# An attention block's opening: x transposed raw, mean and rstd spread by transposes, rstd applied to the first query product

## The chip, the cores and the metric

The kernel runs on one core of a Trainium2 chip. The core has five engines with queues of their own: TensorE (PE; its weight loads are shown apart as PEld), VectorE (DVE), ScalarE (ACT), GpSimd (POOL) and SyncE (SP), which here issues nearly all DMA transfers. Each engine takes its instructions in the order written and waits on semaphores for the others. The metric is the time of one execution on the device in microseconds; runs of the kernel before gave a median of 568.15 us (three runs, 568.02 to 568.37).

## What is computed

Cross attention with a layer norm in front, in float32, for a batch of 8 sequences of 256 rows of width 1024, 32 heads of 32:

```python
mu, var = mean(x), var(x)                       # over the last axis, of 1024
xn = (x - mu) * rsqrt(var + 1e-5) * gamma + beta
Q = split_heads(xn @ Wq.T)                      # 32 heads of 32
K = V = split_heads(ctx)                        # the memory is used for both
probs = softmax(where(mask, Q @ K.T / sqrt(32), -inf))
out = x + merge_heads(probs @ V) @ Wout.T
```

## The kernel before

All shapes are cut into tiles of 128 partitions. A sequence `b` of 256 rows is two halves `s`; the width of 1024 is eight chunks `c` of 128; the query has eight tiles `o` of 128 columns, each holding four heads. The unit of work is `n = 8 * b + o`, 64 in all: a query tile, its scores (four heads, one PSUM bank each, tag `sc`, four banks in all), a softmax, the values, and the output projection of the sequence before. The whole order is written by hand: each engine's queue holds its instructions in the order in which the Python code emits them.

The norm: `ln_stats` (line 217) takes two `bn_stats` of 512 columns and a `bn_aggr` on VectorE, adds epsilon, and raises to the power -0.5 on GpSimd (line 235). `ln_norm` (line 242) subtracts the mean and multiplies by rstd on the rows. PE then transposes the rows (x is the stationary operand, the identity or a diagonal matrix the moving one), since the query product contracts over the width. Gamma and beta differ by column of x, so after the transpose they are one number per partition. The query tile carries one more column (S, the 257th) that holds what beta gives; it serves as the bias of the queries of the later sequences, for which gamma and the scale are folded into `wq` (`fold`, line 364).

The opening, which the change touches, is sequence 0 and stands after line 876:

- 32 dummy transposes of the identity into a spare bank (line 119), before any data are there.
- Loads on SP's queue: rows of half 0 in two pieces, rows of half 1, `wq` tile 0, the keys, the mask, rows of sequence 1, further `wq` tiles; gamma and beta are loaded from ScalarE's queue (line 193).
- Half 0: statistics (line 227); the mean is subtracted by VectorE from the first 512 columns (line 882) and by GpSimd from the rest (line 885); rstd stands in a diagonal matrix (line 884), and the transposes of line 273 are products with that matrix, which apply rstd. `copy_x0` (lines 280 and 282) evacuates them with gamma and beta. `first_q(0)` (line 290) makes the first query tile's half, copied with the scale by line 294.
- Half 1: statistics, `ln_norm` on VectorE (line 253), plain transposes (line 271), the same evacuation, `first_q(1)`.
- The scores of half 0 (line 486), then two chunks of query tile 1 (`make_q`, line 345), then the scores of half 1, then the other chunks of tile 1 and tile 2. VectorE takes maxima with the mask (line 524), ScalarE exponentials (line 528), GpSimd the normalization (line 543). VectorE also takes the statistics of sequence 1 between the two halves' maxima.

Of the kernel before, what the change touches and what calls it, by code (L numbers as in the profile page):

```python
# [46 lines left out]
F32 = mybir.dt.float32  # L47
# [4 lines left out]
P = 128  # L52
# [7 lines left out]
def xattn_kernel(  # L60
# [54 lines left out]


    busy = ps_s.tile([P, P], F32, tag="sc", name="busy")
    for _ in range(32):
        nc.tensor.transpose(busy, ident, ident)


    xs, ks, vs, rs = {}, {}, {}, {}
# [68 lines left out]

    nc.scalar.activation(gs[:, :NS], mhalf, AF.Exp)
    nc.scalar.dma_start(gb, gamma_beta)
    load_x(0, 0, 0)
    load_x(0, 0, 1)
    load_x(0, 1)
    load_wq(0)
    load_k(0)
    load_mask(0)
    load_x(1, 0)  # L200
    load_wq(1)
    load_x(1, 1)
    for o in range(2, 5):
        load_wq(o)
# [12 lines left out]
    def ln_stats(b, s, parts=range(3), later=None):  # L217


        if s == 0 and 0 in parts:  # L220
            mvs[b] = sm.tile([P, NS, 2], F32, tag="mv", name=f"mv_{b}", bufs=2)
            rstds[b] = sm.tile([P, NS], F32, tag="rstd", name=f"rstd_{b}", bufs=2)
        if 0 in parts:
            sts[b, s] = sm.tile([P, 2, 6], F32, tag="st", name=f"st_{b}_{s}", bufs=2)
        for h in range(2):
            if h in parts:
                nc.vector.bn_stats(sts[b, s][:, h, :], xs[b][:, s, ts(h, 512)])
        if 2 not in parts:
            return
        nc.vector.bn_aggr(mvs[b][:, s, :], sts[b, s].rearrange("p h k -> p (h k)"))  # L230
        ve = sm.tile([P, 1], F32, tag="ve", name=f"ve_{b}_{s}", bufs=2)
        nc.vector.tensor_scalar(ve, mvs[b][:, s, 1:2], LN_EPS, None, ALU.add)

        def pow_():
            nc.gpsimd.tensor_tensor(rstds[b][:, s : s + 1], ve, mhalf[:, :1], ALU.pow)

        if later is None:
            pow_()
        else:
            later.append(pow_)  # L240
# [14 lines left out]
            ALU.subtract, ALU.mult,  # L255
        )

    xnT0 = lnp.tile([P, NC, S + 1], F32, tag="xnT", name="xnT_0")
    xnTs[0] = lambda c: xnT0[:, c, :]
    px0 = {}  # L260

    def transpose_x0(s, diag=None):

        pool, tag, k = (ps_v, "pv", NC // 2) if diag is None else (ps_s, "sc", 2)
        for g in range(NC // k):
            pt = pool.tile([P, k, P], F32, tag=tag, name=f"px0_{s}_{g}")
            for i in range(k):
                px0[s, k * g + i] = pt[:, i, :]
                chunk = xs[0][:, s, ts(k * g + i, P)]
                if diag is None:  # L270
                    nc.tensor.transpose(pt[:, i, :], chunk, ident)
                else:
                    nc.tensor.matmul(pt[:, i, :], chunk, diag, start=True, stop=True)  # L273

    def copy_x0(s, c, engine):

        to, pt = xnT0[:, c, ts(s, P)], px0[s, c]
        g, b = gam[:, c : c + 1], bet[:, c : c + 1]
        if engine is nc.scalar:
            nc.scalar.activation(to, pt, AF.Identity, bias=b, scale=g)  # L280
        else:
            nc.vector.tensor_scalar(to, pt, g, b, ALU.mult, ALU.add)

    def first_q(s, chunks=range(NC)):

        if s == 0:
            pqs[0] = ps_q.tile([P, 512], F32, tag="pq", name="pq_0")
        cols = ds(0, P) if s == 0 else ds(P, P + 1)
        for c in chunks:
            nc.tensor.matmul(  # L290
                pqs[0][:, cols], wq[:, 0, c, :], xnT0[:, c, cols],
                start=(c == chunks[0]), stop=(c == chunks[-1]),
            )
        nc.scalar.activation(qa[:, 0, cols], pqs[0][:, cols], AF.Copy, scale=NEG_SCALE)

    xes, px1 = {}, {}

# [51 lines left out]
    def copy_q(n):  # L349
        b, o = divmod(n, NQ)  # L350
        if b == 0:
            nc.scalar.activation(qa[:, o], pqs.pop(n), AF.Copy, scale=NEG_SCALE)
        elif b == 1:
            nc.scalar.activation(
                qa[:, o, :S], pqs.pop(n), AF.Identity, bias=qa[:, o, S : S + 1],
            )
        else:
            nc.scalar.activation(
                qa[:, o, :S].rearrange("p (s a k) -> p a s k", s=NS, a=NA),
                pqs.pop(n).rearrange("p (a s k) -> p a s k", s=NS, a=NA),  # L360
                AF.Identity, bias=qa[:, o, S : S + 1],
            )
# [113 lines left out]
        nc.vector.tensor_scalar(mbs[b], mks.pop(b), 1.0, -MASKED, ALU.subtract, ALU.mult)  # L476

    def scores(n, part=range(NS)):
        if 0 in part:
            scs[n] = [  # L480
                ps_s.tile([P, NS, T], F32, tag="sc", name=f"sc_{n}_{j}") for j in range(NH)
            ]
        for s in part:
            for j in range(NH):
                r = slice(j * HD, (j + 1) * HD)
                nc.tensor.matmul(  # L486
                    scs[n][j][:, s, :], qa[r, n % NQ, ts(s, P)], ks[n - n % 2][r, n % 2, :],
                    start=True, stop=True,
                )
# [10 lines left out]
    def softmax_parts(n, copies=(), ahead=(), between=(), hooks={}, fill=()):  # L500
# [14 lines left out]
        es, mns, dens = {}, {}, {}  # L515

        def exps(j, part=range(NS)):
            if 0 in part:
                es[j] = ep.tile([P, NS, T], F32, tag="e", name=f"e_{n}_{j}")
                mns[j] = sm.tile([P, NS], F32, tag="mn", name=f"mn_{n}_{j}")  # L520
                dens[j] = sm.tile([P, NS], F32, tag="den", name=f"den_{n}_{j}")
# [34 lines left out]

        if n == 0:
            for j in range(NH - 1):
                exps(j, (0,))
            yield  # L560
            exps(NH - 1, (0,))
            fill_in()
            yield
            for j in range(NH):
                exps(j, (1,))
            normalize(0)
            fill_in()
        else:
# [307 lines left out]
                    rings[slot].append(partial(load_ring, name, half))  # L876


    ln_stats(0, 0)
    x0 = xs[0][:, 0, :]  # L880
    mean = mvs[0][:, 0, 0:1]
    nc.vector.tensor_scalar(x0[:, :512], x0[:, :512], mean, None, ALU.subtract)
    diag = ring[:, 0, 1, :]
    nc.vector.tensor_scalar(diag, ident, rstds[0][:, 0:1], None, ALU.mult)
    nc.gpsimd.tensor_scalar(x0[:, 512:], x0[:, 512:], mean, 1.0, ALU.subtract, ALU.mult)  # L885
    ln_stats(0, 1)
    transpose_x0(0, diag)
    early, late = (0, 1, 2, 3, 6, 7), (4, 5)
    for c in early + late:
        copy_x0(0, c, nc.vector if c > 5 else nc.scalar)  # L890
    nc.gpsimd.tensor_copy(xnT0[:, :, S], bet)
    ln_norm(0, 1, nc.vector)
    first_q(0, early + late)
    mask_bias(0)
    transpose_x0(1)
    scores(0, (0,))
    for c in range(NC):
        copy_x0(1, c, nc.scalar if c < NC // 2 else nc.vector)
    first = softmax_parts(0, (partial(copy_q, 1), partial(copy_q, 2)), (), (), {}, [
        partial(ln_stats, 1, 0), partial(ln_stats, 1, 1),  # L900
        partial(ln_norm, 1, 0, nc.vector),
    ])
    next(first)
    first_q(1)
    make_q(1, second=True, chunks=range(2))
    next(first)
    scores(0, (1,))
    make_q(1, second=True, chunks=range(2, NC))
    make_q(2)
    for _ in first:  # L910
        pass
    ln_norm(1, 1, nc.vector)
    nc.gpsimd.tensor_scalar(gs, gam, NEG_SCALE, 1.0, ALU.mult, ALU.mult)
    for o in range(2):
        fold(o)

# [246 lines left out]
```

## Time and profile before

| | |
|---|---|
| median of three runs | 568.15 us (568.02 to 568.37) |
| span of the profiled execution | 566.0 us |
| TensorE busy | 561.4 us |
| VectorE, ScalarE, GpSimd busy | 467.6, 423.4, 394.3 us |
| DMA moved | 119.02 MB, mean 210 GB/s |

The span runs from the first to the last instruction; a run's time also has what lies around it. A row of the profile gives the engine, the line of the kernel, the operation, the tile written and the tile read, shapes, the number of instructions, then busy time and mean duration; after a bar stands the idle time of the engine before it and what ended it. Instructions of an engine overlap, so that a duration is not the distance to the next one. A float32 product is two records on PE, a transpose one.

### The profile page before, as it was taken

The page shows a single profiled execution, that of the slowest core. Times are in us where ns is not written, and L with a number is a line of the kernel's source. Part 1 is how long each engine was busy: PE and PEld are TensorE (multiplying, and loading weights), DVE is VectorE, ACT ScalarE, POOL GpSimd, SP SyncE. Part 2 cuts the span into 40 slices and gives each one's busy share as a digit, 9 for nine tenths or more (in the row PEclk, how much of TensorE's full clock was granted, in tenths as well). Part 3 has the DMA queues.
Part 4 walks back from the last instruction along what each step waited for, and adds up shares of the span by engine and source line. Part 5 has one row for each costly group of instructions (what it writes and reads, how often), then busy time and mean ns, then how long its engine had stood idle before and what let it go on. Part 6 is the DMA issues. An engine that isn't in the chain of part 4 may idle for free.

```text
span 566.0 us, 20200 instructions
## 1 busy us (share of the span) xinstructions
PE 561.4 (99%) x7266; PEld 393.7 (70%) x7266; DVE 467.6 (83%) x1716; ACT 423.4 (75%) x1464; POOL 394.3 (70%) x636
## 2 busy tenths in 40 slices
PE   8999999999999999999999999999999999999997
PEld 8788886767766767667766776667766767755454
DVE  5889889999988988878898888988888777879923
ACT  4699999997778866786777876778776776769820
POOL 2788887899777656857568665777648657448780
PEclk9999999999999999999999999999999999999999
DMA  8966667856697777966778767796658864536751
GB/s 310 397 181 199 185 198 228 281 162 179 212 301 232 223 202 235 263 195 191 233 216 239 215 176 221 230 273 193 176 140 269 255 191 128 146 110 180 218 156 74
DMA packets 47219, 119.02 MB, mean 210 GB/s; under 512 B 8976, under 2 KB 9744, under 8 KB 47120
## 3 DMA queue, kind: packets, MB, share of 16 engines
q1 hardware_dynamic: 46976, 117.74, 69.5%
q8 instruction: 57, 0.93, 0.8%
q14 instruction: 42, 0.34, 0.2%
q10 hardware_dynamic: 144, 0.01, 0.0%
HBM read 66.33 MB, written 11.53 MB: 138 GB/s over the span
## 4 chain that ended last, share of the span: by engine, by line
PE 97%; DMA 1%; DVE 0%; POOL 0%; ACT 0%; issue 0%; SPq 0%; POOLq 0%
PE po_S L720 21%; PE pq_A L447 19%; PE pv L636 12%; PE sc L486 12%; PE po_A L720 11%; PE pq L345 9%; PE pq_S L447 8%; PE po_end L787 3%; PE po_last L787 1%; DMA x<-in_x_dram 1%; PE po_end_s L787 0%; POOL x L885 0%; PE pq L290 0%; PE px L307 0%; ACT e L528 0%; PE px L273 0%
## 5 line engine op out<-in xcount | busy, mean ns | idle before, releaser
L543 POOL TENSOR_SCALAR e<-e,rden 128x256 f32<-128x256 f32 x466 | 215.4, 479 | 125.5 <-DVE rden L535 123.0
L528 ACT ACTIVATE e<-e,mn 128x256 f32<-128x256 f32 x512 | 254.0, 502 | 46.1 <-DVE mn L524 44.9
L549 DVE STREAM_TRANSPOSE pT<-e 128x512 f32<-128x512 f32 x256 | 178.9, 703 | 35.6 <-POOL e L543 27.5
L524 DVE CUSTOM_DVE_ANT_0 e<-sc,mb 128x256 f32<-128x256 f32 x512 | 185.3, 415 | 25.4 <-PE sc L486 25.1
L555 ACT COPY pc<-pT 128x512 f32<-128x512 f32 x128 | 79.0, 617 | 55.7 <-DVE pT L549 35.6
L528 ACT ACTIVATION_READ_ACCUMULATOR e<-e,mn 128x1 f32 x512 | 98.4, 192 | 0.0
L486 PEld LDWEIGHTS sc<-k,qa 32*128 32x128 f32 x1024 | 46.1, 184 | 42.2 <-issue 21.6
L720 PE MATMUL po_S<-wo,at 128*128 128x512 f32 x152 | 74.3, 606 | 0.0
L636 PE MATMUL pv<-pT,v 64*32 64x128 f32 x4096 | 74.1, 274 | 0.0
L486 PE MATMUL sc<-k,qa 32*128 32x256 f32 x1024 | 73.6, 401 | 0.1
L636 PEld LDWEIGHTS pv<-pT,v 64*32 64x32 f32 x4096 | 57.0, 105 | 22.5 <-issue 11.8
L720 PE MATMUL po_A<-wo,at 128*128 128x512 f32 x128 | 59.4, 605 | 0.0
L345 PE MATMUL pq<-xnT,wq 128*128 128x256 f32 (+1 forms) x240 | 55.0, 384 | 0.0
L447 PEld LDWEIGHTS pq_A<-xnT,wq 128*128 128x128 f32 x416 | 48.5, 192 | 6.2 <-issue 4.8
L345 PEld LDWEIGHTS pq<-xnT,wq 128*128 128x128 f32 x240 | 44.6, 190 | 8.2 <-issue 1.5
L720 PE MATMUL po_S<-wo,s 128*128 128x512 f32 x104 | 50.1, 606 | 0.0
L447 PE MATMUL pq_A<-xnT,wq 128*128 128x128 f32 x416 | 48.5, 275 | 0.0
L535 DVE RECIPROCAL rden<-den 128x2 f32<-128x2 f32 x256 | 38.2, 150 | 7.3 <-ACT e L528 6.2
L524 DVE DVE_READ_ACCUMULATOR2_ANT mn<- 128x1 f32 x512 | 42.4, 83 | 0.0
L720 PEld LDWEIGHTS po_A<-wo,at 128*128 128x128 f32 x128 | 22.9, 189 | 25.6 <-issue 24.5
L720 PEld LDWEIGHTS po_S<-wo,at 128*128 128x128 f32 x152 | 25.5, 190 | 19.5 <-issue 19.5
L753 POOL TENSOR_TENSOR r<-r,p 128x512 f32<-128x512 f32 x24 | 30.6, 1277 | 4.8 <-ACT e L528 3.0
(102 smaller groups left out, 666.1 us busy)
## 6 DMA issues: line engine op xcount, KB each, us to landing
v<-in_kv_dram SPq DMA_DIRECT2D x32, 512.0 KB, 4.2
pT<-pT SPq DMA_DIRECT2D x128, 128.0 KB, 2.9
pT<-pc SPq DMA_DIRECT2D x128, 128.0 KB, 4.0
ring<-kept_T SPq DMA_DIRECT2D x20, 512.0 KB, 5.3
k<-in_kv_dram SPq DMA_DIRECT2D x32, 256.0 KB, 4.1
x<-in_x_dram SPq DMA_DIRECT2D x15, 512.0 KB, 5.6
r<-in_x_dram SPq DMA_DIRECT2D x28, 256.0 KB, 4.5
out_dram<-r SPq DMA_DIRECT2D x28, 256.0 KB, 3.2
```

Source lines behind the costliest of these rows:

```text
L345: nc.tensor.matmul(pqs[n], wq[:, o, c, :], xnTs[b](c), start=(c == 0), stop=(c == NC - 1),)
L447: nc.tensor.matmul(pqs[b][:, o, :], w[:, c], x_[:, c], start=begins and o + c == 0, stop=c == NK - 1, skip_group_check=True,)
L486: nc.tensor.matmul(scs[n][j][:, s, :], qa[r, n % NQ, ts(s, P)], ks[n - n % 2][r, n % 2, :], start=True, stop=True,)
L524: nc.vector.tensor_tensor_reduce(out=e[:, s, :], in0=pss[j][:, s, :], in1=mbs[n // NQ], scale=1.0, scalar=NO_SCORE, op0=ALU.add, op1=ALU.m ...
L528: nc.scalar.activation(e[:, s, :], e[:, s, :], AF.Exp, bias=mn[:, s : s + 1], scale=-1.0, accum_out=den[:, s : s + 1],)
L535: nc.vector.reciprocal(rden, dens[j])
L543: engine.tensor_scalar(es[j][:, s, :], es[j][:, s, :], rden[:, s : s + 1], 1.0, ALU.mult, ALU.mult,)
L549: nc.vector.transpose(pT[:, :, :, j, :, :].rearrange("p a i s k -> p (a i) s k"), es[j].rearrange("p s (b t) -> p b s t", t=K),)
L555: nc.scalar.copy(pc[:, :, ts(j, 2)], pT[:, 1, :, ts(j, 2)])
L636: nc.tensor.matmul(pvs[n][r][j * HD : (j + 1) * HD], vs[n - n % 2][ts(r, 2 * K), i, ds(n % 2 * P + j * HD, HD)], pT[ts(r, 2 * K), :, i, j, ...
L720: nc.tensor.matmul(po, operand(b, name)[:, c], wo[:, which, c], start=begins and c == 0, stop=c == NK - 1, skip_group_check=not begins,)
L753: nc.gpsimd.tensor_tensor(r, r, p1s[b], ALU.add)
```

## The change

The opening of sequence 0 is written anew:

- The half s=1 is loaded, normalized and used first, then s=0. The second `wq` tile is loaded ahead of the rows of sequence 1.
- Of the 32 dummy transposes 6 stay at the start; 10 more stand in groups of 2, 2, 3 and 3 between the real ones.
- The rows are transposed as they land, without mean or rstd. A column of 128 means (or rstds), read with its one column repeated 128 times, is transposed as well (`spread`): each partition then holds the row of all means. ScalarE copies it out of PSUM (`keep_mean`, `keep_rstd`) into a buffer that is free until later (`sums_x`).
- VectorE subtracts the means while it takes the transposed rows out of PSUM, 512 columns at a time (`centre_x0`). Gamma with the negative scale is multiplied in place, 16 chunks of 128x128, twelve by ScalarE and four by VectorE (`gamma_x0`). This is `xcT0`.
- The first query product (`first_q`) reads `xcT0`, so rstd is still missing; `take_q` multiplies the product by the row of rstds on VectorE and adds the bias on ScalarE. For the other query tiles `scale_x0` makes `xnT0` from `xcT0` times rstd, three quarters of it on GpSimd and one on VectorE.
- `copy_q` of sequence 0 becomes two ScalarE instructions: the bias column, and the queries with that bias. The scale factor `gs` is computed at the start instead of ahead of the folds.

The diff, cut to its core:

```diff
-    for _ in range(32):
-        nc.tensor.transpose(busy, ident, ident)
+    def keep_busy(times):
+        for _ in range(times):
+            nc.tensor.transpose(busy, ident, ident)
+    keep_busy(6)
...
-    load_x(0, 0, 0)
-    load_x(0, 0, 1)
-    load_x(0, 1)
+    load_x(0, 1, 0)
+    load_x(0, 1, 1)
+    load_x(0, 0)
     load_wq(0)
     load_k(0)
     load_mask(0)
+    load_wq(1)
     load_x(1, 0)
-    load_wq(1)
     load_x(1, 1)
...
+    rows = sums_x.rearrange("p i c a k -> p (i c a k)")
+    rows0, means0 = rows[:, :S], rows[:, ds(S, S)]
+    def transpose_x0(s, g):
+        px0[s, g] = ps_v.tile([P, NC // 2, P], F32, tag="pv", name=f"px0_{s}_{g}")
+        for i in range(NC // 2):
+            chunk = xs[0][:, s, ts(NC // 2 * g + i, P)]
+            nc.tensor.transpose(px0[s, g][:, i, :], chunk, ident)
+    def spread(s, what):
+        if what == 0:
+            stat0[s] = ps_o.tile([P, 2, P], F32, tag="po", name=f"stat0_{s}")
+        one = mvs[0][:, s, 0:1] if what == 0 else rstds[0][:, s : s + 1]
+        nc.tensor.transpose(stat0[s][:, what, :], one.to_broadcast([P, P]), ident)
+    def keep_mean(s):
+        nc.scalar.copy(means0[:, ts(s, P)], stat0[s][:, 0, :])
+    def centre_x0(s, g):
+        nc.vector.tensor_tensor(
+            xcT0[:, ts(g, NC // 2), ts(s, P)], px0[s, g],
+            means0[:, ts(s, P)].unsqueeze(1).to_broadcast([P, NC // 2, P]), ALU.subtract,
+        )
+    def gamma_x0(s, c, engine):
+        it, g = xcT0[:, c, ts(s, P)], gs[:, c : c + 1]
         if engine is nc.scalar:
+            nc.scalar.activation(it, it, AF.Copy, scale=g)
         else:
+            nc.vector.tensor_scalar(it, it, g, None, ALU.mult)
+    def keep_rstd(s):
+        nc.scalar.copy(rows0[:, ts(s, P)], stat0[s][:, 1, :])
+    def scale_x0(s, g, engine):
+        engine.tensor_tensor(
+            xnT0[:, ts(g, NC // 2), ts(s, P)], xcT0[:, ts(g, NC // 2), ts(s, P)],
+            rows0[:, ts(s, P)].unsqueeze(1).to_broadcast([P, NC // 2, P]), ALU.mult,
+        )
+    QUERY_0 = (0, 1, 2, 3, 4, 6, 5, 7)
...
+    def take_q(o, bank, cols):
+        to = qa[:, o, cols]
+        nc.vector.tensor_tensor(to, bank[:, cols], rows0[:, cols], ALU.mult)
+        nc.scalar.activation(to, to, AF.Identity, bias=qa[:, o, S : S + 1])
...
-            nc.scalar.activation(qa[:, o], pqs.pop(n), AF.Copy, scale=NEG_SCALE)
+            bank = pqs.pop(n)
+            take_bias(o, bank)
+            nc.scalar.activation(
+                qa[:, o, :S], bank[:, :S], AF.Identity, bias=qa[:, o, S : S + 1],
+            )
...
+    def gammas(s):
+        for c in QUERY_0:
+            gamma_x0(s, c, nc.vector if s == 0 and c in (2, 4, 6, 7) else nc.scalar)
+    nc.gpsimd.tensor_scalar(gs, gam, NEG_SCALE, 1.0, ALU.mult, ALU.mult)
+    for to in (xcT0, xnT0):
+        nc.gpsimd.tensor_scalar(to[:, :, S], bet, NEG_SCALE, 1.0, ALU.mult, ALU.mult)
+    ln_stats(0, 1)
+    transpose_x0(1, 0)
+    keep_busy(2)
+    transpose_x0(1, 1)
+    keep_busy(2)
+    spread(1, 0)
+    keep_busy(3)
+    spread(1, 1)
+    keep_busy(3)
+    keep_mean(1)
+    keep_rstd(1)
+    centre_x0(1, 0)
+    centre_x0(1, 1)
+    gammas(1)
+    scale_x0(1, 0, nc.gpsimd)
     ln_stats(0, 0)
+    scale_x0(1, 1, nc.gpsimd)
+    transpose_x0(0, 0)
+    transpose_x0(0, 1)
+    first_q(1, QUERY_0[:5])
+    spread(0, 0)
+    first_q(1, QUERY_0[5:])
+    spread(0, 1)
+    keep_mean(0)
+    centre_x0(0, 0)
+    centre_x0(0, 1)
+    take_bias(0, pqs[0])
+    gammas(0)
+    keep_rstd(0)
+    take_q(0, pqs[0], slice(P, S))
+    scale_x0(0, 0, nc.vector)
+    scale_x0(0, 1, nc.gpsimd)
     mask_bias(0)
+    first_q(0)
+    scores(0, (1,))
+    take_q(0, pqs[0], slice(0, P))
...
-    first_q(1)
     make_q(1, second=True, chunks=range(2))
     next(first)
-    scores(0, (1,))
+    scores(0, (0,))
     make_q(1, second=True, chunks=range(2, NC))
     make_q(2)
```

64 lines of the change are left out of this document (16 added, 48 removed).

## The prediction

> **What bounds the kernel now.** I read the page first, then busy time by stretches, then the chain of waits in order of time. The page says that TensorE (PE) works nearly all of the span and that the chain that ends last is PE too.
>
> ```profile
> span 566.0 us, 20200 instructions
> PE 561.4 (99%) x7266; PEld 393.7 (70%) x7266; DVE 467.6 (83%) x1716; ACT 423.4 (75%) x1464; POOL 394.3 (70%) x636
> PE 97%; DMA 1%; DVE 0%; POOL 0%; ACT 0%; issue 0%; SPq 0%; POOLq 0%
> ```
>
> By stretches (columns: stretch, its length, busy us and records of PE, weight loads, VectorE, ScalarE, GpSimd, then granted clock, DMA share, GB/s):
>
> ```profile
> 0.00:20.00 20.00, 18.26 (x125) 16.10 (x126) 13.88 (x45) 10.17 (x31) 5.99 (x15) 1.00 0.90 339
> 20.00:100.00 80.00, 80.00 (x1005) 61.46 (x1005) 71.15 (x276) 72.25 (x242) 69.54 (x95) 1.00 0.73 221
> ```
>
> From 20 us on PE has no gap. The edit touches only what comes before that, so its worth is the time by which the gapless run of PE begins earlier or later. The chain shows where that run begins (start, us, what):
>
> ```profile
> 4.22 0.70 DVE st L227
> 4.95 0.22 DVE mv L230
> 5.20 0.16 DVE ve L232
> 5.50 0.65 POOL rstd L235
> 6.16 2.00 POOL x L885
> 8.20 1.16 PE px L273 x8
> ...
> 15.38 0.17 ACT qa L294
> 15.60 0.71 PE sc L486 x8
> 16.31 6.28 PE pq L345 x28
> ```
>
> Statistics, rstd, subtraction, transposes, two query products and the scores of the first head (the rows left out): then from 16.24 (the weight load of that last row, quoted below) one long PE run. Two terms that PE waits for go: the 2.00 us subtraction on GpSimd, and the wait for the second query copy before 15.60.
>
> **The clock under the opening.** Half of the answer lies in what the 32 dummy transposes do now. The same view for line 119 alone (PE and weight loads only):
>
> ```profile
> 1.34:4.84 3.50, 3.49 (x17) 3.50 (x18) 1.00 0.85 276
> 4.84:6.54 1.70, 1.70 (x17) 1.65 (x15) 1.00 1.01 345
> ```
>
> 18 loads in 3.50 us are 0.19 us each, 15 in 1.65 us 0.11: the spacing nearly halves at about 4.8 us, 3.5 us after PE began, while the column of the granted clock says 1.00 in both. [...]
>
> The edit replaces 32 dummies in a row by 6, then 2, 2, 3, 3 between real transposes. PE then works from 1.34 to 2.5, waits for x until some 3.4 (2.6 after its issue, quoted below) and goes on with short gaps: of the first 3.5 us some 2.6 are busy instead of all. So the turn may come at 4.8 as now, or up to one stretch (3.5 us) later, at 8.2. I carry both.
>
> **Prices.** Rows for what the new path is made of, weight loads for PE (a line's spacing is its span over its loads):
>
> ```profile
> 9.08 1.87 PEld L290 LDWEIGHTS pq<-xnT,wq 128*128 128x128 f32 x16
> 10.90 0.87 PEld L271 LDWEIGHTS px<-ring,x 128*128 128x128 f32 x8
> 15.60 0.31 PEld L486 LDWEIGHTS sc<-k,qa 32*128 32x128 f32 x8 [0.49 <-ACT qa L294]
> 16.24 5.95 PEld L345 LDWEIGHTS pq<-xnT,wq 128*128 128x128 f32 x28 [0.33 <-issue]
> 30.07 0.91 ACT L538 ACTIVATE e<-e,rden 128x256 f32<-128x256 f32 x2
> 105.88 1.13 ACT L457 ACTIVATE qa<-pq_S,qa 128x128 f32<-128x128 f32 x4
> L649 ACT COPY at<-pv 128x128 f32<-128x128 f32 x128 | 26.1, 253 | 8.9 <-PE pv L636 8.9
> L762 DVE TENSOR_TENSOR r<-po_S,r 128x512 f32<-128x512 f32 x18 | 12.1, 675 | 0.2
> 6.83 1.27 DVE L227 BATCH_NORM_STATS2 st<-x 128x6 f32<-128x512 f32 x2
> 5.27 0.48 DVE L882 TENSOR_SCALAR x<-x,mv 128x512 f32<-128x512 f32 x1
> L696 POOL TENSOR_TENSOR at<-at 128x512 f32<-128x512 f32 x8 | 10.2, 1272 | 0.0
> ```
>
> A query product of one chunk is two records: 0.235 us at 128 columns, 0.425 at 257 (28 loads in 5.95 us are 14 products). A transpose is 0.12 at the fast rate and lands 0.27 after its start. Four scores hold PE 0.64 (15.60 to 16.24). A 128x128 copy from PSUM on ScalarE is 0.25. The in-place gamma multiplication there (128x128, SBUF, a scale read per partition) does not occur: two 256-wide ones take 0.91, four 128-wide ones from PSUM 1.13, so one follows the other after 0.26 (line 457) to 0.40 (line 538); I take 0.295, nearer to the narrow one, and 0.4 for the last to land. Centring is the 0.675 of line 762. VectorE's gamma multiplication is 0.2 to 0.3, under the 0.48 of four times its width. GpSimd's multiplication by rstd is 1.28.
>
> **The new opening step by step**, with the turn at 4.84:
> - Statistics of s=1 come first, rows loaded in the place that s=0 had: mean at 5.10, ve 5.30, rstd 5.95 as in the chain above.
> - PE: 12 transposes and dummies end by 5.3; the mean is spread from 5.36 and lands 5.63; copied to 5.92. Centring 5.96 to 6.63 and to 7.24. The spread rstd is copied by 6.56.
> - ScalarE, eight gammas: 6.67 + 7 x 0.295 = 8.74, landing 9.13. This is the new long pole.
> - VectorE meanwhile: statistics of s=0, mean 8.66, ve 8.85. PE: eight transposes to 7.7, then query products behind the gammas, five by 8.94; the mean of s=0 spread to 9.21 (it is queued behind those five, and the last three are queued behind it); product finished 9.93.
> - ScalarE copies that mean to 9.51; centring to 10.21 and 10.82; first gamma 10.25 to 10.65. The other product starts at 10.69, eight chunks at 0.235 to 12.6. The gammas, split over two engines, keep ahead of it.
> - Scores of s=1 at 12.63 (their query scaled by rstd on VectorE, bias on ScalarE, ready 12.38), 0.64; two chunks of the next query, 0.85; scores of s=0 at 14.12 (query ready 13.56), 0.64. The remaining chunks start at 14.76 against 16.24: 1.48 us earlier.
>
> With a turn anywhere from 6 to 7 us the same steps end 0.41 later (gain 1.07), since the twelve slow transposes delay the mean and the copies behind it; with a turn at 8.2, 0.84 later (gain 0.64).
>
> What this hangs on besides: wq's first tile and gamma.
>
> ```profile
> 0.72 1.33 SPq L129 DMA_DIRECT2D x<-in_x_dram  x3
> DMA to landing us min/median/max: 2.6/5.0/8.4
> 1.00 0.38 ACTq L193 DMA_DIRECT2D gb<-in_gamma_beta_dram  x1
> 2.10 0.43 SPq L166 DMA_DIRECT2D wq<-in_wq_dram  x1
> DMA to landing us min/median/max: 5.6/10.1/11.1
> ```
>
> The first row is three x loads, the second of all x loads up to 12 us, the last of all wq loads. At the least 5.6 after its issue, the first lands at 7.7, where the new product starts; it had landed by 9.08, where the old one starts without a wait. At 9.08 the gain is 0.17 instead of 1.48. I take 7.7: this load is the earliest in the queue. Gamma now heads GpSimd's queue, before rstd, in three small operations (0.52 us for the one moved from 23.50). At the least that an x load took, 2.6 us, it lands at 3.6 and they end at 5.2, in time; if it lands at 5.0 the gain falls to 0.67. The second wq load now goes ahead of an x load of b=1 on the same queue, 0.5 MB at the 339 GB/s of the first stretch, an estimated 1.5 us; the statistics of that x are due only at 14.4.
>
> **What is late next.** PE's earlier arrival must not meet banks still being read. The score banks are reused two heads on:
>
> ```profile
> 17.37 0.42 DVE L524 CUSTOM_DVE_ANT_0 e<-sc,mb 128x256 f32<-128x256 f32 x1
> 26.95 0.41 DVE L524 CUSTOM_DVE_ANT_0 e<-sc,mb 128x256 f32<-128x256 f32 x1
> 28.15 1.15 PE L486 MATMUL sc<-k,qa 32*128 32x256 f32 x16
> 23.50 0.52 POOL L913 TENSOR_SCALAR gs<-gb 128x8 f32<-128x8 f32 x1
> ```
>
> VectorE leaves the last bank at 27.36; PE asks for it some 0.4 (three of the four scores of a half) after 28.15: 1.2 us of slack. VectorE's own chain gains less than PE, since the statistics of the next x (1.27 of line 227, 0.38 of the two after it) sit between its two sets of four maxima, 0.35 each: by the steps above the first set starts at 13.07 and the second ends at 17.44, which is 0.35 before the 17.79 of now (17.37 + 0.42); at a middle turn 0.07 after it. So up to 1.2 + 0.35 or 1.2 - 0.07 us can be kept, which just covers 1.48 and 1.07. At the head after, GpSimd gains the 0.52 of line 913 as well. ScalarE pays an extra one-column copy per query tile of the first sequence, seven times; it has idle time there (72 of 80 us busy).
>
> **Sum.** Between 1.07 and 1.48 I take 1.25, about the middle, since neither turn has a row: 566.0 - 1.25 = 564.75 for the span of the profiled execution. The runs' median of 568.15 lies 2.15 above that span, so 566.9.
>
> **Rivals.**
> (a) The clock turns only after real products. The dummies then fail to do their work: the product of s=1 starts near 8.3, and a turn one stretch of 3.5 us after it is 11.8. Steps at the slow rate (0.46 per chunk) end 1.0 us later than now, and VectorE's maxima 2.15 later, which less the slack of 1.2 is 1.0: as both hold PE at different places, I take 1.3 slower, 569.45. For it: PE stands still for 0.9 us early and waits in between; against it: dummies alone sufficed before. It is a loss from a turn at about 9.6 on. [...]
> (b) GpSimd and VectorE get in each other's way.
>
> ```profile
> 6.15 2.00 POOL L885 TENSOR_SCALAR x<-x,mv 128x512 f32<-128x512 f32 x1
> 6.19 0.72 DVE L884 TENSOR_SCALAR ring<-ring,rstd 128x128 f32<-128x128 f32 x1 [0.45 <-POOL rstd L235]
> 20.68 2.74 POOL L543 TENSOR_SCALAR e<-e,rden 128x256 f32<-128x256 f32 x6
> ```
>
> Line 543 does 512 columns in 0.91, line 885 beside VectorE took 2.00, and VectorE's 128 columns 0.72, more than the 512 of line 882. The new kernel runs four such multiplications beside GpSimd's multiplication by rstd. At 0.65 each the scores of s=1 wait and the gain is gone: 568.25. Against it: that GpSimd operation may be over by 11.2, and VectorE's begin at 10.8. [...]
> (c) The gain dies at the score banks, or wq comes late: PE stands still before the third head's scores. 567.9.
> (d) All goes better, gammas at 0.26 or less, and shorter waits: 1.9 us, 566.25.
>
> **Chances.** Forecast (gain 0.6 to 1.6) 0.60; (a) 0.16; (b) 0.09; (c) 0.07; (d) 0.08. This kernel's measurement tells 0.2%, 1.14 us, from no change. Above that: 0.39 of the forecast's 0.60, and (d): 0.47. Slower by that much: nearly all of (a) and a little of (b), 0.17. The rest, 0.36, is within. The likeliest case alone reaches from 566.5 to 567.5; the range, taking in (b), (c) and the lighter half of (a) and part of (d), is 566.2 to 569.0.
>
> **What would show it.** Right: weight loads of the first transposes at 0.19 and of the product of s=1 at 0.117 or so; the gammas on ScalarE 0.3 apart from 6.7 on; the long PE run from about 15.0; no PE gap before the third head's scores. Wrong: products of s=1 at 0.19 per record (then (a)); VectorE's gammas at 0.6 or more (b); products waiting for wq, or rstd of s=1 after 6.5 for gamma (c). A change after 30 us of more than 0.3 us would refute the view that the opening alone decides.

## The result, and the profile after

The changed kernel takes 575.09 us (median of four runs, 573.93 to 575.86) against 568.24 (568.02 to 568.37, four runs) of the kernel before: a ratio of 1.0117 with a 95% interval of 1.0103 to 1.0132. The forecast was 1.25 us faster; it is 6.85 us slower, outside the range. The profiled execution is the slowest of the four, 575.86, so spans below differ by more than the medians.

The page of the changed kernel, with the rows that answer to those of before (busy time of each engine, and the clock in slices):

```profile
span 574.0 us, 20189 instructions
PE 563.7 (98%) x7246; PEld 394.3 (69%) x7246; DVE 468.3 (82%) x1718; ACT 426.3 (74%) x1478; POOL 397.9 (69%) x639
PEclk9799999999999999999999999999999999999999
```

The span grew by 8.0 us (from 566.0) and PE's busy time by only 2.3. So PE stands still some 5.7 us more and also works longer for the same products. The second digit of the clock, a 7, says why the work is longer: within slice 2 (14.4 to 28.7 us) the clock was reduced. By stretches (length, PE busy and records, granted clock, DMA share, GB/s):

```profile
11.00:12.00 1.00, 0.95 (x7) 1.00 1.06 434
13.00:14.00 1.00, 0.00 (x0) 0.92 1.05 426
14.00:15.00 1.00, 0.29 (x1) 0.50 1.01 408
...
20.00:21.00 1.00, 1.00 (x4) 0.67 1.02 406
```

PE has nothing to do from 11.95 to 14.71. A mean of 0.92 in the stretch from 13 is half a clock for its last 0.16 us, so the clock halves at about 13.84, 1.9 us into the standstill; 0.67 from 20 puts its return at 20.66. In between PE works for 6 us, from 14.71, at half rate. The mean granted clock of this execution is 0.994, which such a fall of 6.8 us explains; in the other three it is 0.996 to 0.997, so there too it falls, by an estimate from these means for 3 to 5 us. What the fall costs below is the price in this execution, where it lasts longest.

The timeline of the opening (start, us, engine, line, what; in brackets the idle time before it and what ended that):

```profile
5.01 0.69 DVE L231 BATCH_NORM_STATS2 st<-x 128x6 f32<-128x512 f32 x1 [0.79 <-DMA x<-in_x_dram]
7.12 0.27 PE L282 MATMUL stat<-ring,rstd 128*128 128x128 f32 x1
7.43 0.27 ACT L285 COPY sx<-stat 128x128 f32<-128x128 f32 x1 [5.21 <-PE stat L282]
8.52 2.45 ACT L296 ACTIVATE xcT<-xcT,gs 128x128 f32<-128x128 f32 x8 [0.66 <-DVE xcT L288]
10.68 0.27 PE L282 MATMUL stat<-ring,mv 128*128 128x128 f32 x1
11.63 0.32 PE L282 MATMUL stat<-ring,rstd 128*128 128x128 f32 x1
11.99 0.27 ACT L285 COPY sx<-stat 128x128 f32<-128x128 f32 x1 [1.02 <-PE stat L282]
13.01 1.28 ACT L296 ACTIVATE xcT<-xcT,gs 128x128 f32<-128x128 f32 x4 [0.70 <-DVE xcT L288]
13.49 0.87 DVE L298 TENSOR_SCALAR xcT<-xcT,gs 128x128 f32<-128x128 f32 x4
14.27 0.28 DVE L325 TENSOR_TENSOR qa<-pq,sx 128x128 f32<-128x128 f32 x1
14.71 3.75 PE L317 MATMUL pq<-xcT,wq 128*128 128x128 f32 x16 [2.75 <-DVE qa L325]
21.79 6.35 PE L380 MATMUL pq<-xnT,wq 128*128 128x257 f32 x28
```

The long PE run begins at 21.79 instead of 16.24: 5.55 of the 8.0 us. Two rows show waits for nothing that the waiting instruction reads. The mean of half 0 lies in PSUM at 10.95 (10.68 + 0.27), yet ScalarE copies it at 11.99, right behind the spread of rstd (11.63 + 0.32), which stands in the same PSUM tile. And the second product, whose first gamma multiplication starts at 13.01 on ScalarE and has landed by 13.4 (0.39 each), starts at 14.71, behind VectorE's reading of the other columns of its own bank (14.27 + 0.28).

Two more losses come later. First the kernel before (ScalarE's copy out of the single PSUM bank of tag `pq` that the query tiles here share, called the query bank below, then PE's next query product into it), then the changed kernel (ScalarE, PE, GpSimd):

```profile
28.86 0.36 ACT L352 ACTIVATE qa<-pq 128x257 f32<-128x257 f32 x1
29.27 3.75 PE L345 MATMUL pq<-xnT,wq 128*128 128x257 f32 x16
...
171.46 1.88 PE L720 MATMUL po_S<-wo,s 128*128 128x512 f32 x4
```

```profile
35.34 0.13 ACT L329 COPY qa<-pq 128x1 f32<-128x1 f32 x1
35.51 0.48 ACT L389 ACTIVATE qa<-pq,qa 128x256 f32<-128x256 f32 x1
36.04 3.75 PE L380 MATMUL pq<-xnT,wq 128*128 128x257 f32 x16 [1.00 <-ACT qa L389]
...
177.17 1.27 POOL L792 TENSOR_TENSOR r<-r,p 128x512 f32<-128x512 f32 x1 [3.35 <-DMA r<-in_x_dram]
179.22 1.98 PE L759 MATMUL po_S<-wo,s 128*128 128x512 f32 x4 [0.91 <-DVE r L801]
```

At 36.04 PE waits for the one query bank that ScalarE has still to empty. In the kernel before, the same sixteen records start at 29.27: from 5.55 the lag grows to 6.77. At 179.22 it waits for a residual that came in late by DMA (row at 171.46 before): 7.76. The last 0.2 is spread over the rest.

### The profile page after: what moved, and what is told of

Its sections match the earlier page's. It is cut to its first block, busy times and chain, and to the rows that moved or that the text cites. A ratio compares the mean times of both kernels' runs of the same rounds, so it can differ in the third digit from the quotient of the medians.

```text
span 574.0 us, 20189 instructions
## 1 busy us (share of the span) xinstructions
PE 563.7 (98%) x7246; PEld 394.3 (69%) x7246; DVE 468.3 (82%) x1718; ACT 426.3 (74%) x1478; POOL 397.9 (69%) x639
## 4 chain that ended last, share of the span: by engine, by line
PE 90%; DMA 3%; DVE 3%; ACT 1%; POOL 1%; SPq 1%; issue 1%; DVEq 0%; POOLq 0%; ACTq 0%
PE po_S L759 19%; PE pq_A L486 18%; PE pv L675 11%; PE sc L525 11%; PE po_A L759 9%; PE pq L380 8%; PE pq_S L486 7%; PE po_end L826 3%; PE po_last L826 1%; DMA r<-in_x_dram 1%; ACT e L567 1%; PE pq L317 1%; DVE e L563 1%; DMA pT<-pT 1%; POOL e L582 1%
```

## The experiments

Theory 1: the two waits through shared PSUM tiles, and the standstill that they cause, with the clock that falls in it, are most of the loss. Rivals: the short dummy run (6 in place of 32) leaves PE at half rate for long, as the prediction's case (a) feared; the extra ScalarE copies; the order of the loads. The last has no run of its own below; in the changed kernel's trace the statistics of sequence 1, whose rows now come behind the second `wq` tile, start at 21.02 without a wait for them.

### The standstill filled with dummies (gap_dummies)

```diff
     spread(0, 1)
+    keep_busy(24)
```

> The changed kernel with 24 dummy transposes behind the spread of the second rstd row, where TensorE stood still from 11.9 to 14.7 us. Theory (two waits on shared PSUM tiles make TensorE stand still, and the standstill halves its clock from 13.9 to 20.5 us): the waits stay, so the second product still starts near 14.7, but the granted clock stays 1.00; the stretch from 14.7 to 20.5 takes half, the long run of TensorE begins near 18.9 instead of 21.8, and the time is near 572. Rival (the new path is simply long, and the halved clock is hidden behind the slow vector work): the long run begins no more than 0.5 us earlier, 574.5 or more.

Measured: 572.9 us, ratio to before 1.0084 (1.0062 to 1.0106). Its PE timeline, and one stretch of it:

```profile
12.12 2.78 PE L121 MATMUL busy<-ring 128*128 128x128 f32 x24
15.04 2.02 PE L317 MATMUL pq<-xcT,wq 128*128 128x128 f32 x16
...
19.87 6.35 PE L380 MATMUL pq<-xnT,wq 128*128 128x257 f32 x28
```

```profile
11.00:20.00 9.00, 8.86 (x71) 1.00 1.03 411
```

With work that produces nothing the clock stays at 1.00, and the sixteen records take 2.02 us instead of 3.75, although they start 0.33 later. From the product's start to the long run it is 4.83 us instead of 7.08: 2.25 us is what the halved clock costs. From 12.12 to 14.9 PE does nothing but these transposes, so in this run transposes alone held the clock up (1.00 from 11 to 20 us, against 0.50 from 13.84 without them). The long run still starts 1.0 later than the 18.9 expected.

### The mean copied before rstd is spread (mean_early)

```diff
     spread(1, 0)
+    keep_mean(1)
     keep_busy(3)
     spread(1, 1)
     keep_busy(3)
-    keep_mean(1)
...
     spread(0, 0)
+    keep_mean(0)
     first_q(1, QUERY_0[5:])
     spread(0, 1)
-    keep_mean(0)
```

> The changed kernel with the copy of the mean row emitted ahead of the spread of the rstd row, for both halves, so that the copy no longer waits for the second write into the same PSUM tile. Theory: the first copy comes at 6.8 instead of 7.4, the second 1 us sooner after the first shift, the second product starts some 1.6 us earlier (its wait for the scaled first product stays), TensorE stands still for under 2 us and may keep its clock: 570 to 573.5. Rival (the copy is late for other reasons, the gammas on ScalarE): no shift above 0.3 us, 574.5 or more.

Measured: 572.87 us, 1.0081 (1.0059 to 1.0103). ScalarE and PE:

```profile
10.47 0.27 ACT L285 COPY sx<-stat 128x128 f32<-128x128 f32 x1
...
13.22 1.02 PE L317 MATMUL pq<-xcT,wq 128*128 128x128 f32 x7 [1.79 <-DVE qa L325]
```

The copy follows the mean's own transpose (10.16 + 0.27) directly, without the 1.02 us, so that wait was the order of the instructions on one tile, not the data. (The x7 counts only the records inside this view's window; a row at a window's end is shortened so.) PE's standstill is 1.79 us, and the clock stays at 1.00 in all stretches of this profile. In two of the other three executions its mean is 0.997, so it falls somewhere in them; no trace shows where. PE still waits for VectorE's reading of its bank.

### A bank of its own for the second half's query product (own_bank)

```diff
+        if s == 0:
+            pqs["half"] = ps_v.tile([P, 512], F32, tag="pv", name="pq_0_0")
+        bank = pqs["half"] if s == 0 else pqs[0]
         for c in chunks:
             nc.tensor.matmul(
-                pqs[0][:, cols], wq[:, 0, c, :], xcT0[:, c, cols],
+                bank[:, cols], wq[:, 0, c, :], xcT0[:, c, cols],
...
-    take_q(0, pqs[0], slice(0, P))
+    take_q(0, pqs["half"], slice(0, P))
```

> The changed kernel with the second half's query product in a PSUM bank of its own, so that it no longer waits for the scaled copy of the first half out of the shared bank. Theory: the second product starts at the first gamma, near 13.4 instead of 14.7, TensorE stands still 1.5 us instead of 2.75, and if the clock holds the long run begins near 17.6: about 570. If the clock falls all the same, 573.5. Rival (the product waits for its gammas, not for the bank): the product starts at 14.5 or later, 574.5 or more.

Measured: 572.41 us, 1.0077 (1.0054 to 1.01). PE:

```profile
13.96 2.12 PE L320 MATMUL pq<-xcT,wq 128*128 128x128 f32 x16 [1.52 <-ACT xcT L296]
19.14 6.35 PE L383 MATMUL pq<-xnT,wq 128*128 128x257 f32 x28
```

The product no longer waits for VectorE (qa) but for the first gamma (xcT), its data. With a standstill of 1.52 the clock does not fall, and its mean is 1.00 in all four executions. The long run was expected near 17.6 and the time near 570: in this profile the clock first turned at about 9.8 (7.0 in the changed kernel), the mean's copy still waits some 0.8 us for rstd's spread (mean in PSUM at 11.66, copied at 12.48), and the second set of scores is slow (1.49 us, see the next run).

### Both waits away (both_waits)

The two edits above together.

> The changed kernel with both waits taken away (mean copied ahead of the rstd spread, the second half's product in a bank of its own). Theory: the second product starts near 11.9, TensorE stands still for 1 us at most, the granted clock stays 1.00, the long run begins near 16.2, and the time is 568 to 569.5, level with the kernel before or little above. Rival (the new path is itself longer than the old one by 5 us): 572 or more.

Measured: 570.72 us, 1.0039 (1.0026 to 1.0052). PE:

```profile
12.46 2.12 PE L320 MATMUL pq<-xcT,wq 128*128 128x128 f32 x16 [0.73 <-ACT xcT L296]
14.52 0.71 PE L528 MATMUL sc<-k,qa 32*128 32x256 f32 x8
16.23 1.49 PE L528 MATMUL sc<-k,qa 32*128 32x256 f32 x8
17.65 6.35 PE L383 MATMUL pq<-xnT,wq 128*128 128x257 f32 x28
```

The time lies between the theory's 568 to 569.5 and the rival's 572. Of the loss of 1.17%, 0.39 are left, where each of the two edits alone left 0.81 and 0.77. The long run starts 4.14 us earlier than in the changed kernel, not the 3.74 and 2.65 of the two together (6.39): each alone already keeps the clock at 1.00 in its profile, so its 2.25 is in both; mean_early then lost more behind the opening (three waits of 1.0 to 1.1 us of PE in its trace, two of 1.0 and 0.5 here). Of the rest, these rows show a third meeting in a bank: the second set of scores takes 1.49 us for the same records as the first set's 0.71. They go into the other half of the same four score banks, which VectorE is reading for the first half's maxima at that time (15.50 to 17.0). In the changed kernel the second set starts at 21.15, when these maxima are over (21.10), and takes 0.71. And the wait for the query bank, 1.00 us before 31.89, is still there, so it isn't a consequence of the two waits in the opening.

### The dummies alone, in the kernel before (before_six)

```diff
-    for _ in range(32):
+    for _ in range(6):
```

> The kernel before with 6 dummy transposes at the start instead of 32, nothing else. Theory (TensorE's clock turns only after some 3.5 us or more of work, so cutting the dummies alone makes real work slow): the transposes of line 273 and the first product run at 0.19 us per weight load instead of 0.12, the long run of TensorE begins 1 to 2.5 us later than 16.24, and the time is 569.2 to 571. Rival (the clock matters little in the opening, which waits for vector work): within 0.4 us of the kernel before. Side reading: if the first x rows land at 3.5 to 3.9 and the second at 4.5 or later here too, the dummies and not the order of the rows set that; if they land at 3.4 and 4.2, the dummies do not.

Measured: 571.07 us, 1.0038 (1.002 to 1.0055). Weight loads, then PE:

```profile
6.90 3.49 PEld L273 LDWEIGHTS px<-ring,x 128*128 128x128 f32 x16 [4.41 <-DVE ring L884]
...
18.75 6.35 PE L345 MATMUL pq<-xnT,wq 128*128 128x257 f32 x28
```

In the kernel before, the 26 dummies are worth 2.5 us of the long run's start: with 6, weight loads are 0.22 apart from 6.90 to past 12, after 4.41 us without one, where in the kernel before they are 0.12 apart. Here VectorE also waits 1.11 us for the second half of x (its statistics start at 7.96; 6.83 in the kernel before), so not all of the 2.5 need be the clock's.

### Twelve dummies at the start (first12)

```diff
-    keep_busy(6)
+    keep_busy(12)
```

(on top of both waits away)

> The changed kernel with both waits taken away and 12 dummy transposes at the start instead of 6, so that TensorE works without a gap until x lands. Theory (the gap of 1 us at 2.5 us holds the clock's turn back from 4.8 to 8 or 9): the weight loads fall to 0.11 us apart before 7 us, the row of means is ready some 0.3 to 0.6 us earlier, and the time is 0.3 to 1 us below that with 6 dummies (570.7), 569.7 to 570.4. Rival (the turn hangs on the real products or on chance): the turn stays at 7 to 9.5 us and the time within 0.3 us of 570.7.

Measured: 569.88 us, 1.0019 (1.0007 to 1.0031), against 1.0039 with six; the two intervals just overlap. In this profile weight loads come down to 0.12 apart at about 6.8 us (9.4 with six). PE's long run and the wait:

```profile
17.22 6.35 PE L383 MATMUL pq<-xnT,wq 128*128 128x257 f32 x28
31.46 1.79 PE L383 MATMUL pq<-xnT,wq 128*128 128x257 f32 x7 [1.01 <-ACT qa L392]
```

### The mask's bias early, the next statistics late (mended)

On top of first12, the mask's bias is made right after the statistics of half 0, and the statistics of sequence 1 only after both sets of maxima.

```diff
             exps(NH - 1, (1,))
-            fill_in()
             yield
...
     ln_stats(0, 0)
+    mask_bias(0)
...
     scale_x0(0, 1, nc.gpsimd)
-    mask_bias(0)
     first_q(0)
```

> The changed kernel with both waits taken away, 12 dummies first, the mask bias moved ahead of the centring of the second half (out from beside GpSimd's multiplication, where it took 1.27 us), and the statistics of the next sequence moved behind the second set of maxima. Theory (what is left of the loss is VectorE's and ScalarE's chain, later by 2.2 us, which the third query's bank waits for): the second set of maxima begins near 16.3, TensorE's wait before the fourth query product falls from 1 us to under 0.4, and the time is 567.8 to 569. Rival (the rest lies in the opening on TensorE itself): 569.7 or more.

Measured: 570.13 us, 1.0019 (1.0007 to 1.0032): no gain. PE:

```profile
4.89 0.47 PEld L275 LDWEIGHTS px<-ring,x 128*128 128x128 f32 x4
8.93 1.35 PE L320 MATMUL pq<-xcT,wq 128*128 128x129 f32 x10 [0.20 <-DMA wq<-in_wq_dram]
```

In this run the clock turned before 4.9 (0.12 per load), and then wq's first tile was the last to come: it lands at about 8.9, where the prediction took 7.7. The long run starts at 17.47, and PE's wait at the query bank is 0.72, where under 0.4 was expected. The mask's bias did not get away from GpSimd either: it waits for the mask's load, starts at 10.23 beside GpSimd's multiplication by rstd (10.12 to 11.30), and takes 1.22 us.

### Two ScalarE copies in place of one, in the kernel before (before_copies)

```diff
-            nc.scalar.activation(qa[:, o], pqs.pop(n), AF.Copy, scale=NEG_SCALE)
+            bank = pqs.pop(n)
+            nc.scalar.activation(qa[:, o, S : S + 1], bank[:, S : S + 1], AF.Copy, scale=NEG_SCALE)
+            nc.scalar.activation(qa[:, o, :S], bank[:, :S], AF.Copy, scale=NEG_SCALE)
```

> The kernel before with each query copy of the first sequence split into two ScalarE instructions as in the changed kernel (the bias column, then the 256 others). Theory (TensorE has no slack at the single query bank at 29.3 us, so whatever ScalarE is late there TensorE is late): the fourth query product starts 0.2 to 0.5 us later, and the time is 568.5 to 569.1. Rival (the copies lie in idle time, as the prediction had it): within 0.2 us of the kernel before.

Measured: 568.58 us, 0.9991 (0.9978 to 1.0004). ScalarE, at the same place as above:

```profile
28.79 0.15 ACT L353 ACTIVATE qa<-pq 128x1 f32<-128x1 f32 x1
28.84 0.36 ACT L354 ACTIVATE qa<-pq 128x256 f32<-128x256 f32 x1
```

These copies cost nothing. But they are not yet those of the changed kernel. Here the two do not depend on each other, start 0.05 apart, and ScalarE's next instruction follows 0.31 us after the first (at 29.10), against 0.27 for the one copy before (28.86 to 29.13). In the changed kernel the second copy adds the column that the first writes: it starts 0.17 behind it, and the next instruction follows after 0.54 (35.34 to 35.88). So the rival of the extra copies is not settled by this run.

### The query copies ahead of the third exponentials (first12_copy)

On top of first12:

```diff
             exps(2)
+            if n == 1:
+                for copy in copies:
+                    copy()
+                copies = ()
             normalize(0)
             exps(3)
```

> first12 with one move: in the softmax of the second query tile, ScalarE issues the copies of the next query ahead of the third quarter of exponentials instead of behind it. Theory: PE's wait of 1.0 us before the query product at 31.5 is ScalarE's lateness at the only query bank; it goes, nothing of it comes back before the end of the first sequence, and the time falls 0.7 to 1.0 under first12: 569.0. Rival: the wait only moves on to the score banks, since VectorE and ScalarE are just as late for the exponentials then put off; 569.7 to 570.

Measured: 569.84 us, 1.0017 (1.0006 to 1.0028), against first12's 569.88: no gain, so the theory of this step fails as to the time, and the rival's 569.7 to 570 holds. The next kernel has the same edit, and its trace shows where the wait went.

### The mask's bias behind the query of half 0 (mask_late)

```diff
-    mask_bias(0)
     first_q(0)
     scores(0, (1,))
     take_q(0, pqs["half"], slice(0, P))
+    mask_bias(0)
```

(on top of first12_copy)

> first12_copy with the bias of the mask made behind the query of half 0 on VectorE instead of ahead of it. Theory: the 1.27 us of the mask's bias stand ahead of the query of half 0, so its scores come later and the long PE run with them; behind it, the run starts 0.3 to 0.5 earlier than in first12 (17.2), the time is 568.5 to 569.0. Rival: the scores of half 0 wait for the banks of half 1's scores and the maxima that read them, which now come later still, so the run starts no earlier and the time is first12_copy's or above.

Measured: 569.95 us, 1.0025 (1.0015 to 1.0035). PE:

```profile
11.32 2.12 PE L320 MATMUL pq<-xcT,wq 128*128 128x128 f32 x16 [0.51 <-ACT xcT L296]
...
15.09 1.52 PE L528 MATMUL sc<-k,qa 32*128 32x256 f32 x8
16.54 6.35 PE L383 MATMUL pq<-xnT,wq 128*128 128x257 f32 x28
...
29.80 3.74 PE L383 MATMUL pq<-xnT,wq 128*128 128x257 f32 x16
...
46.28 2.01 PE L383 MATMUL pq<-xnT,wq 128*128 128x257 f32 x8 [0.24 <-ACT qa L392]
...
173.47 1.98 PE L766 MATMUL po_S<-wo,s 128*128 128x512 f32 x4 [0.65 <-DVE r L808]
```

Two readings. The long run starts 0.68 ahead of first12's, but the second product already does by 0.69 (11.32 against 12.01), before the moved instruction, in a profile whose clock turned at about 4.6 instead of 6.8: the move itself gained nothing, and the second scores take 1.52 as before. The rival of this run held. And the wait of 1.01 at the query bank is gone (29.80, without one), but 0.24 of it stands at the next pair of query copies, and 0.65 at the residual. At 29.80 this kernel is 0.53 behind the kernel before (29.27), at 46.28 it is 0.97 behind, and at 173.47 2.01 behind (45.31 and 171.46 there). What is won in the opening is lost again to resources that have little slack in the kernel before: ScalarE's turn at the query bank (its copy ends at 29.22, PE goes on at 29.27), and the residual (VectorE's addition ends at 171.13, PE goes on at 171.46). On ScalarE each query copy now is two instructions, 0.54 us up to the next instruction in place of 0.27 (29.10 to 29.64 here, 28.86 to 29.13 before), and from 27.6 to 46 us ScalarE is busy for 18.27 of 18.40 us, while in the kernel before it has 0.37, 0.17 and 0.28 us ahead of single exponentials there. So the copies of the changed kernel may well cost something here; no run takes them away alone.

### Which rows are fetched first (before_swap, late_swap)

In every run of the changed order the first half of x lands later than in the kernel before, by the same loads on the same queue. The first test: the kernel before with the rows of the two halves of sequence 0 exchanged in the loads of x. The residual and the stores keep their rows, so the output of sequence 0 is not the reference's.

```diff
-        nc.sync.dma_start(xs[b][:, s, cols], x[b, ts(s, P), cols])
+        row = 1 - s if b == 0 else s
+        nc.sync.dma_start(xs[b][:, s, cols], x[b, ts(row, P), cols])
```

> The kernel before with the two halves of sequence 0 fetched from each other's rows; queue, order and sizes of the loads stay as they are, and the outputs of sequence 0 belong to swapped query rows. Theory (which rows are fetched sets when they land): the two pieces of the first half land as in the changed kernel and its variants, at 3.5 to 3.9 and 4.5 to 5.0 us instead of 3.4 and 4.2, and the long PE run starts 0.3 to 0.8 later than 16.2. Rival (the queue beside them sets it, the second half's rows or the short dummy run): they land at 3.4 and 4.2, and the long run starts at 16.2.

VectorE, and PE's long run:

```profile
3.72 0.69 DVE L228 BATCH_NORM_STATS2 st<-x 128x6 f32<-128x512 f32 x1 [3.72 <-DMA x<-in_x_dram]
4.80 0.69 DVE L228 BATCH_NORM_STATS2 st<-x 128x6 f32<-128x512 f32 x1 [0.39 <-DMA x<-in_x_dram]
...
16.83 6.36 PE L346 MATMUL pq<-xnT,wq 128*128 128x257 f32 x28
```

The pieces land at 3.7 and 4.8 instead of 3.4 and 4.2, and the long run starts 0.59 later. The one time, 568.68, is too coarse for that. The reverse, on top of mask_late: rows 0 to 127 in the place of half 1, for loads of x, loads of the residual and stores alike.

```diff
-        nc.sync.dma_start(xs[b][:, s, cols], x[b, ts(s, P), cols])
+        nc.sync.dma_start(xs[b][:, s, cols], x[b, ts(1 - s if b == 0 else s, P), cols])
...
-        nc.sync.dma_start(rs[b, s, h], x[b, ts(s, P), ts(h, 512)])
+        nc.sync.dma_start(rs[b, s, h], x[b, ts(1 - s if b == 0 else s, P), ts(h, 512)])
...
-        nc.sync.dma_start(out[b, ts(s, P), ts(h, 512)], r)
+        nc.sync.dma_start(out[b, ts(1 - s if b == 0 else s, P), ts(h, 512)], r)
```

> mask_late with the rows of sequence 0 swapped throughout: half 1 of the kernel holds rows 0 to 127 (loads of x, loads of the residual and stores alike), so that the rows that land first are again those that the kernel before fetches first; the outputs are the reference's. Theory (the rows fetched first set when they land): the first pieces of x land at 3.4 and 4.2 us instead of 3.7 and 4.7, the first statistics end 0.5 earlier, and the long PE run starts 0.2 to 0.5 ahead of mask_late's 16.5, the time 0.2 to 0.5 under mask_late's 569.95, no faster than before. Rival (the lateness belongs to the queue behind: the order of the other loads, or the early short dummy run): landing and time as in mask_late.

Measured: 570.7 us, 1.0037 (1.0024 to 1.0051). VectorE, then PE:

```profile
3.40 1.34 DVE L231 BATCH_NORM_STATS2 st<-x 128x6 f32<-128x512 f32 x2 [3.40 <-DMA x<-in_x_dram]
```

```profile
8.14 1.06 PE L275 MATMUL px<-ring,x 128*128 128x128 f32 x8 [1.26 <-DMA x<-in_x_dram]
...
17.59 6.35 PE L383 MATMUL pq<-xnT,wq 128*128 128x257 f32 x28
```

The landing follows the rows: 3.40, and both pieces without a gap between. With that the first statistics end 0.9 earlier than in mask_late, but now the second half is late: PE waits 1.26 us for it at 8.14, and the long run starts 1.05 later than mask_late's. In time it is no gain (570.7 against 569.95, with intervals that overlap). The theory held for the landing and failed for its worth.

No version of the changed kernel beats the kernel before; first12, first12_copy and mended come nearest, at 1.0017 to 1.0019.

## Why the prediction was wrong

**The step that failed** is the ledger of the new opening. It let every step start when its data were there and its engine free. Its landmarks, with the later turn of the clock that the prediction allowed for (0.41; the measured one lies at about 7), stand so against the trace:

| step | predicted, with 0.41 | measured | growth of the lag | what added it |
|---|---|---|---|---|
| mean of half 1 copied | 6.33 | 7.70 | 1.4 | second piece of x lands at 5.01, not 4.22; the copy waits for rstd's spread too |
| last gamma of half 1 | 9.54 | 10.97 | 0.1 | as forecast: 8 in 2.45 us, 0.3 apart |
| mean of half 0 copied | 9.92 | 12.26 | 0.9 | the same wait for rstd's spread |
| second product starts | 11.10 | 14.71 | 1.3 | waits for VectorE's reading of its bank |
| long PE run | 15.17 | 21.79 | 3.0 | half clock, 2.25; of the other 0.8, gap_dummies has 0.5 in its second scores (1.24 for 0.71), behind maxima |

So the instructions were priced about right, and what was missing lay between them. Two waits of 1.02 and about 1.3 us come from instructions that share a PSUM bank and not a byte of data. The experiments show both as such: the copy moves up to its data when the order is changed (mean_early: data at 10.43, copy at 10.47), the product when the bank is (own_bank: at 13.96, ended by the first gamma). The ledger allowed for neither. These rows do not tell waits by bank from waits by tile, for the instructions of each wait meet in one tile.

One row was read short as well: the ledger has rstd at 5.95, where the chain's row gives 6.15 (5.50 + 0.65). Beside the rest this is small.

**The clock** was carried as one question, when it first turns. It turns late, but not at 11.8 as case (a) has it: weight loads come down from 0.22 apart to 0.12 at about 7. That a late turn comes by 8.2, one stretch behind the 4.8 of before, was the author's estimate: no run shows such a bound, and in own_bank the loads come down only at about 9.8. What costs 2.25 us in the profiled execution is a second fall, after 1.9 us of a standstill. The prediction knew of gaps, but its gaps were short; with the bank waits the gap grew to 2.75 and took the clock along. The effect of case (a), a product at half rate, came by another road.

**What is late next** was named as the score banks, with 1.2 us of slack, and as "at the head after" GpSimd. The score banks cost PE at most 0.2 there (a set of scores of 1.33 us where 1.15 is usual). The place with no slack is ScalarE's copy out of the one query bank: in the kernel before it ends at 29.22 and PE goes on at 29.27. The prediction put the extra copies there at nothing because ScalarE has idle time in the 80 us. In the changed kernel's trace it has next to none where it matters (busy for 5.10 of the 5.13 us from 30.87 to 36.0), and a query copy takes 0.27 us more of it. What that term is worth in time stays open, since before_copies has the cheaper pair.

**The claim that the opening alone decides** falls by its own test: 1.22 us more appear at 36 us and 0.9 at 179.

**wq** was taken at 7.7, the early end; the one run whose product waited for it shows 8.9, near the late end, 9.08. By the prediction's own working (1.48 at 7.7, 0.17 at 9.08) this alone would cut the gain to about 0.3. In the changed kernel's own trace the first product, at 9.56, does not wait for `wq`.

**Right were** the prices of the gammas on ScalarE (0.295 forecast, 2.45 for eight) and on VectorE (0.87 for four, not case (b)'s 0.65 each) and of the centring (1.29 for two). What case (b) feared does show in an operation that it did not name: the mask's bias takes 1.27 us (15.08 to 16.35) while GpSimd multiplies by rstd (busy until 16.2), 0.55 in mask_late, where GpSimd is done 0.4 after its start, and 0.29 in the kernel before, with GpSimd idle.

Of the loss of 1.17%, both waits with their clock are 0.78 and six more dummies at the start 0.20, by ratios to the kernel before; the second figure is not clear of noise, since the two intervals overlap. The remaining 0.19 (0.07 to 0.31) is not settled: scores behind maxima in shared banks (0.8 in the trace), the landing of x, ScalarE's dearer copies at the query bank and the residual's DMA all appear in the traces, but taking one away let another appear, and the time did not move.

## What to carry to other kernels

When costing a new order by hand, give each PSUM tile a row of its own beside the engines, and let an instruction start when its data are there, its engine is free, and every earlier access to that tile by another engine has ended, even at other columns: the two waits that this would have put into the ledger here are 1.02 and about 1.3 us. Ask of every gap left on PE not only how long it is but whether the clock falls behind it (here it did in one of 2.75, and not in those of 1.52 and 1.79 that were profiled); transposes that fill it were cheap: with 24 of them the product here started 0.33 us later and took 1.73 less. Slack is read at the place where the engine behind the bottleneck hands its bank over, not from that engine's share of the span.

## What the hardware showed that was not expected

The granted clock fell 1.9 us into a standstill of 2.75 and stayed at 0.50 for 6.8 us, the last 6 of them with PE at work; standstills of 1.52 and 1.79 us in the profiles of own_bank and mean_early left it at 1.00, though two unprofiled executions of mean_early have a mean of 0.997. The three turns of this trace, at about 7.0, 13.84 and 20.66, lie 6.8 us apart each time; what sets that distance, no run here shows. The first of them is read from the spacing of weight loads alone: 0.22 us before it, as at the granted 0.50 later (16 in 3.49), and 0.12 behind it, while the granted clock says 1.00 on both sides. By that spacing the first turn lay between 7.0 and 9.8 us in five kernels of the changed order with 6 dummies at the start, and between 4.6 and 6.8 in four with 12, though in each group the first 5 us are nearly the same instructions; so half a microsecond in the start of the long run, seen in one profile, says nothing of an edit. The rows that a load fetches changed its landing: the first piece of rows 0 to 127 of the first sequence lands at 3.37 to 3.50 and the second by 4.0 to 4.2, that of rows 128 to 255 by the same instructions at 3.52 to 3.90 and 4.7 to 5.0 (in own_bank by 4.6), in two swaps and all other runs; why, no run here shows.
